# Products of a graph layer from four-pass f32 to three one-pass products, with the order of the engines planned anew

## The chip, the core and the metric

The kernel runs on one core of a Trainium2 chip. The metric is the time in microseconds (us) that the device takes for one execution. A core has five engines with instruction streams of their own: TensorE (PE in the profile; its weight loads are PEld), VectorE (DVE), ScalarE (ACT), GpSimd (POOL) and SyncE (SP, which here only issues transfers). Sixteen DMA engines move data between the device's memory and the core's on-chip memory. Products are summed in the eight banks of PSUM.

## What is computed

One layer of a graph network over 625 nodes with 512 features and 20,625 edges of four relations:

```
h = relu(layernorm(x))                                    # no gain, no bias
msg[e] = (h[src[e]] @ W_rel[type[e]] + b_rel[type[e]]) * w[e]
agg[n] = sum of msg[e] over dst[e] = n, / max(sum of w[e], 1)
x1 = layernorm(h + h @ W_self + b_self + agg) * g1 + b1
y  = x1 + gelu(x1 @ W_ffn1 + b_ffn1) @ W_ffn2 + b_ffn2
out = x + layernorm(y) * g2 + b2
```

All in f32. W_rel is 4 matrices of 512x512, W_self one, W_ffn1 is 512x1024 and W_ffn2 1024x512.

## The kernel before

The nodes stand in 5 blocks of 125 (128 partitions). The work has these stages, each in the profile under the lines given:

- **Splitting the input.** Each block of x is normalized on DVE (L645 to L651), turned by TensorE (L305) and copied to `hT` (L676). The scale of the normalization, `rx`, is left out here and multiplied in when a product is taken from PSUM.
- **Products.** For each relation and each block, `product` (L706) multiplies `hT` by the four 128-row pieces of the relation's matrix `raw[r, k]`, four f32 tiles of 128x128 by 128x512 into one bank; an f32 tile shows as two matmul records. `evict` (L711, ACT) scales the result into the row tile `kept[c]`, and `store_rows` (L337, L338, SP) writes it to `table` in the device's memory. W_self is a fifth relation, `r = R`, with the identity added to it (L698, DVE), and `own_row` (L714, DVE) takes its result, with b_self added, into `z`.
- **Where the edges are.** DVE and indirect transfers find, for each node, the place of its edges in the sorted list (L402 to L539).
- **Blocks 0 to 2** are summed by matrices: `slot_hots` (L578 to L583, DVE) builds bf16 one-hot tiles, `slot_sums` (L594, TensorE) turns them into a weight matrix from the 20 groups of table rows to nodes, `empty_sums` (L600, DVE) takes that from PSUM to `sums_w`, and `chunk_sum` (L937) multiplies it in f32 with the 20 tiles `kept`.
- **Blocks 3 and 4** are summed by gathering: POOL issues 70 gathers of 128 table rows (L818) and 12 more (L872); DVE adds six gathered tiles to a seventh (L842), the sum is cut in a high and a low part (L828 ACT, L832 DVE), and TensorE adds both parts to the nodes by a one-hot matrix in fp32r (L862, L863).
- **Second half.** Statistics of `z` (L968), the power on POOL (L300), `normed` (L974, DVE), turning (L305) and `copy_x1` (L982, ACT, with g1 and b1). The residual is `scaled_z` and `shifted_z` (L985, L988; DVE for blocks 0 to 2, POOL for the others), with b_ffn2 added into the row of b1 (L805). Then, for blocks 0 and 1 together, 2 and 3 together, and 4, the first matrix (L1039), the gelu (L1043, ACT), the second (L1048), the sum and statistics (L1066, L1067), the last scaling and the addition of x and b2, and the store (L1020, L1022).

The order is planned while the program is built. Each piece of work is an `op` with its engine, an assumed duration in us, what it comes after, buffer tokens that it takes and gives, a rank and a lag. `Plan.times` walks through time and gives each engine, whenever it is free, the ready piece of lowest rank; what comes out is each engine's fixed order of instructions. On the chip the engines run these orders in turn, and each waits where its data or buffers are late. Transfers in the plan before have a fixed lag (`lag=2.2` after a load, `LAND = 3.2` after a gather). The gathers come after all stores (`all_stored`), and have `MS = 10` buffers. A rank's first number decides: 0 to 1 for what others wait for, 2 for the products, 3 for the chunk sums, 4 for the last matmuls.

On-chip memory is in 51 row tiles of 128x512 f32 and some larger tiles with tags: `xs` holds the input, then the weight matrix of block 2, then x again for the last addition; `T` and `T1` hold `hT` and later `x1T`; `rows` holds index windows and later the rows of g1, b1, g2 and b2; `w1` and `w2` hold small work tiles and later W_ffn1 and W_ffn2.

Of the kernel before, what the change touches and what calls it, by code (L numbers as in the profile page):

```python
# [68 lines left out]
class Plan:  # L69
# [8 lines left out]
    def op(self, engine, us, fn, after=(), take=(), give=(), lag=0.08, rank=None, order=False, level=None, at=0.0):  # L78
# [3 lines left out]
        if engine == "PE":  # L82
            o.lag = max(lag, self.behind)
        o.after = [(a, a.us if order and a.engine == engine else a.us + (0.0 if a.engine == engine == "PE" else a.lag))
                   for a in after if a is not None]
# [15 lines left out]
    def times(self):  # L101
# [4 lines left out]
        while left:  # L106
# [4 lines left out]
            for o in left:  # L111
                if o.least > t + 1e-6 or free.get(o.engine, 0.0) > t + 1e-6 or any(buffers[k] < o.take.count(k) for k in o.take):
                    continue
                if any(a.at is None or a.at + d > t + 1e-6 for a, d in o.after):
# [13 lines left out]
            if not can:  # L128
                times = [e[0] for e in back] + list(free.values()) + [o.least for o in left]
                times += [max(a.at + d for a, d in o.after) for o in left  # L130
# [6 lines left out]
def gnn_layer(ctx, tc, x, edges, edge_groups, firsts, fourths, windows, w_self, w_rel, w_ffn1, w_ffn2, brel_in, rows_in, cols_in, out, n_edges):  # L137
# [30 lines left out]
    ROWS = 51  # L168

# [30 lines left out]
    brel_4 = const.tile([P, D], F32R, name="brel_4")  # L200
    cols = const.tile([P, KF + 2 * KD], F32, name="cols")
    bf1, g1_T, b1_T = cols[:, :KF], cols[:, KF:KF + KD], cols[:, KF + KD:]
    bself_bc, bf2_bc = row("bself"), row("bf2")
# [10 lines left out]
    raw = {}  # L214
# [52 lines left out]
    def node_constants():  # L267
        place = work.tile([P, 1], F32, tag="place", name="place", bufs=1)
        nc.gpsimd.iota(place, pattern=[[0, 1]], base=0, channel_multiplier=1, allow_small_or_imprecise_dtypes=True)
        nc.gpsimd.memset(node_f, 2.0 * N)  # L270
        nc.gpsimd.memset(xw, -1.0)
# [38 lines left out]
    rx = const.tile([P, NB, 1], F32, name="rx")  # L310
# [166 lines left out]
    def load_brel():  # L477
        for q in range(4):
            nc.sync.dma_start(brel[q * Q:q * Q + R], brel_in[:, :D])
# [6 lines left out]
    def relation_degrees():  # L486
# [7 lines left out]
        nc.vector.tensor_copy(deg_4[:, :, :, :R], deg.unsqueeze(2).to_broadcast([P, INNER, 4, R]))  # L494
# [111 lines left out]
    PARTS = ()  # L606
    ORDER = (0, 1, 2, 3, R)
    MS = 10
    WARM = 10
    GATHER = 1.25  # L610
    LAND = 3.2
    SLACK = 1.2
    LATER = 0.3
    G = 4
    X_AT = [3.55, 5.4, 9.0, 10.7, 10.7]
# [5 lines left out]
    plan = Plan(dict(ps=8, add=3, acc=1, one=2, oh=3, low=2, raw=6, row=ROWS - 7, ms=MS, es=6, ow=4, gT=6), free=dict(SP=9.0), behind=0.6)  # L621
# [6 lines left out]
    op("POOL", 0.7, row_constants, after=[hot_consts], rank=(3, 0), at=9.0)  # L628
# [23 lines left out]

    def x_norm_first(k):
# [5 lines left out]
    def x_root(i):  # L659
        nc.gpsimd.tensor_tensor(rx[:, i, 0:1], mv_x[i][:, 2:3], half, op=ALU.pow)  # L660

    for i in range(NB):
# [4 lines left out]
        else:  # L667
            pieces = [op("DVE", 0.5, lambda i=i: x_norm(i), after=[s], rank=(0, i))]
            z_made[i] = pieces[0]
        root_x[i] = op("POOL", 0.55, lambda i=i: x_root(i), after=[z_made[i]], rank=(0, i))  # L670
# [10 lines left out]
    for n, r in enumerate(ORDER):  # L681
        for k in range(KD):
            if r == 0:
                w_at[r, k] = op("DMA", 0.0, None, at=W_AT[k])
            else:
                w_at[r, k] = op("SP", 0.95, lambda r=r, k=k: load_w(r, k), take=["raw", "row"], lag=2.2, rank=(1, n))
        if n == 1:
            ed_at = op("SP", 1.3, lambda: nc.sync.dma_start(ed, edges), rank=(1, 0.5), lag=2.2)
            brel_at = op("SP", 0.3, load_brel, rank=(1, 2.2), lag=2.2)
            brel_high = op("ACT", 0.65, lambda: nc.scalar.copy(brel_4, brel), after=[brel_at], rank=(2, 0))  # L690
            brel_split = op("DVE", 0.65, low_brel, after=[brel_high], rank=(2, 0))
            op("SP", 0.4, bias_rows, rank=(1, 3.2))
            bself_at = op("SP", 0.9, lambda: load_rows(bself_bc, 5, 6), rank=(1, 3.3), lag=2.2)
            bf2_at = op("SP", 0.9, lambda: load_rows(bf2_bc, 4, 5), rank=(1, 4.4), lag=2.2)
            cols_at = op("SP", 0.1, lambda: nc.sync.dma_start(cols, cols_in), rank=(1, 4.5), lag=2.2)

    def added_ident(k):
        nc.vector.tensor_add(raw[R, k][:, k * P:(k + 1) * P], raw[R, k][:, k * P:(k + 1) * P], ident)  # L698

    ident_w = [op("DVE", 0.2, lambda k=k: added_ident(k), after=[w_at[R, k]], rank=(0.8, k)) for k in range(KD)]  # L700
# [7 lines left out]
    def evict(i, r, box):  # L708
        c = r * NB + i
        new_rows(c)  # L710
        nc.scalar.activation(kept[c][:NG], box["p"][:NG], AF.Copy, scale=rx[:NG, i, 0:1])  # L711

    def own_row(i, box):
        nc.vector.scalar_tensor_tensor(z[:, i, :], box["p"], rx[:, i, 0:1], bself_bc, op0=ALU.mult, op1=ALU.add)  # L714

    own, stored, made_row, used = {}, {}, {}, {}
    for n, r in enumerate(ORDER):
        for i in range(NB):
            box, m = {}, None
            last = i == NB - 1  # L720
            for k0, k1 in ((0, 2), (2, 4)) if (r, i) != (0, 0) else [(k, k + 1) for k in range(KD)]:
                needs = [w_at[r, k] for k in range(k0, k1)] if r != R else [ident_w[k] for k in range(k0, k1)]
                needs += [turned_h[j] for j in turned_h if j[0] == i and (i or j[1] <= k1)]
                m = op("PE", 0.86 * (k1 - k0), lambda i=i, r=r, k0=k0, k1=k1, box=box: product(i, r, k0, k1, box),
                       after=[m, *needs], take=["ps"] if k0 == 0 else [],
# [560 lines left out]
```

## Time and profile before

| | us |
|---|---|
| Median of 3 runs (lowest to highest) | 250.5 (250.49 to 251.59) |
| The profiled execution's own time | 252.5 |
| Its span, from first to last instruction | 250.7 |
| PE busy | 236.6 |
| PEld busy | 131.6 |
| DVE busy | 186.7 |
| ACT busy | 53.7 |
| POOL busy | 130.0 |

Busy time is the union of an engine's instructions. Issuing a transfer from SP isn't counted as busy; an indirect transfer issued by POOL is. The span lies 1.8 us under the execution's own time. The mean granted clock of TensorE over the span is 0.99. A row of the timeline has the start, the length, the engine, the line, the operation, what it writes and reads, how many instructions were merged, and in brackets the idle time before it with what ended it.

### The profile page before, as it was taken

How to read it: one execution, taken by the hardware profiler on the slowest of the kernel's cores; microseconds unless marked ns; L12 is line 12 of the kernel's file. 1: busy time of each engine (PE TensorE's matmuls, PEld its weight loads, DVE VectorE, ACT ScalarE, POOL GpSimd, SP SyncE). 2: the span in 40 equal slices, each digit the busy share in tenths (PEclk: the TensorE clock that was granted, in tenths of full speed). 3: DMA queues.
4: the chain of work that ended last, by engine and by line, in shares of the span. 5: the costliest groups of instructions: out<-in, count | busy, mean ns of one | idle time of the engine just before them, and what ended most of it. 6: DMA issues, size and time to landing. Idle time of an engine off the chain costs nothing. (4 is left out here: it accounts for less than half of the span.)

```text
span 250.7 us, 2873 instructions
## 1 busy us (share of the span) xinstructions
PE 236.6 (94%) x893; PEld 131.6 (52%) x893; DVE 186.7 (74%) x392; ACT 53.7 (21%) x105; POOL 130.0 (52%) x153
## 2 busy tenths in 40 slices
PE   6999989999999999997999999999999999899980
PEld 2554444556555554543444444448954588446850
DVE  7997599999999999958979777887767773222032
ACT  2423242121111111010212201305431331302400
POOL 6487103000000008777778778878777889944400
PEclk9999999999999999999999999999999999999996
DMA  6877931789421214699776766669877650201101
GB/s 219 309 256 189 304 104 46 241 292 343 121 91 41 82 43 117 186 332 394 242 213 199 207 199 176 177 180 324 264 204 214 195 165 0 82 0 41 43 3 45
DMA packets 17991, 43.15 MB, mean 172 GB/s; under 512 B 3002, under 2 KB 3748, under 8 KB 17844
## 3 DMA queue, kind: packets, MB, share of 16 engines
q0 software_dynamic: 7024, 22.27, 29.9%
q1 hardware_dynamic: 10546, 20.32, 24.5%
q10 hardware_dynamic: 402, 0.34, 0.5%
q8 instruction: 8, 0.13, 0.2%
q14 instruction: 11, 0.09, 0.1%
HBM read 36.51 MB, written 6.52 MB: 172 GB/s over the span
## 5 line engine op out<-in xcount | busy, mean ns | idle before, releaser
L818 POOL DMA_INDIRECT ms<-table,row_i x70 | 70.1, 1001 | 73.3 <-DMA table<-m 53.1
L706 PE MATMUL pt<-w,hT 128*128 128x512 f32 x200 | 89.8, 596 | 0.0
L706 PEld LDWEIGHTS pt<-w,hT 128*128 128x128 f32 x200 | 36.6, 191 | 38.9 <-issue 37.5
L937 PE MATMUL acc<-m,sums_w 126*128 126x512 f32 x120 | 53.2, 593 | 0.0
L842 DVE SCALAR_TENSOR_TENSOR ea<-ms,wgt_g,ea 128x512 f32<-128x512 f32 x59 | 43.8, 752 | 12.0 <-DMA ms<-table,row_i 11.3
L937 PEld LDWEIGHTS acc<-m,sums_w 126*128 126x128 f32 x120 | 22.5, 190 | 25.0 <-issue 24.4
L1039 PE MATMUL pu<-x1T,w_sb 128*128 128x250 f32 (+1 forms) x192 | 35.4, 341 | 0.0
L1048 PE MATMUL po<-w_sb,gT 128*125 128x512 f32 (+2 forms) x96 | 35.0, 521 | 0.0
L1039 PEld LDWEIGHTS pu<-x1T,w_sb 128*128 128x128 f32 x192 | 31.5, 191 | 4.4 <-issue 1.9
L600 DVE TENSOR_REDUCE sums_w<-bank 126x160 f32<-126x480 f32 x48 | 28.0, 652 | 0.0
L711 ACT ACTIVATE m<-pt,rx 125x512 f32<-125x512 f32 x20 | 13.8, 688 | 59.8 <-PE pt L706 57.1
L1048 PEld LDWEIGHTS po<-w_sb,gT 128*125 128x125 f32 x96 | 16.8, 188 | 16.3 <-issue 13.8
L1066 DVE TENSOR_TENSOR y<-po,z 125x512 f32<-125x512 f32 (+2 forms) x6 | 3.6, 603 | 23.8 <-PE po L1048 23.8
L594 PEld LDWEIGHTS <-w_first 128*128 128x128 bf16 x192 | 14.0, 147 | 6.4 <-issue 5.6
L583 DVE TENSOR_TENSOR w_first<-eqs,turned 128x640 bf16<-128x640 bf16 x36 | 15.5, 487 | 0.4
L824 ACT ACTIVATE ea<-ms,ed 128x512 f32<-128x512 f32 x10 | 6.9, 694 | 39.4 <-DMA ms<-table,row_i 39.4
L1043 ACT ACTIVATE gT<-pu,cols 128x250 f32<-128x250 f32 (+1 forms) x24 | 10.1, 433 | 21.2 <-PE pu L1039 16.8
L578 DVE TENSOR_TENSOR w_first<-turned,grid 128x2000 bf16<-128x2000 bf16 x12 | 14.3, 1194 | 0.0
L594 PE MATMUL bank<-w_first 128*128 128x120 bf16 x192 | 14.0, 225 | 0.0
L872 POOL DMA_INDIRECT ms_first<-table,x_row x12 | 12.1, 1012 | 3.7 <-issue 3.0
L828 ACT CAST eh<-ea 128x512 fp32r<-128x512 f32 x9 | 5.3, 586 | 34.8 <-DVE ea L842 34.8
L300 POOL TENSOR_TENSOR mv_y<-mv_y,half 125x1 f32<-125x1 f32 x5 | 2.8, 562 | 14.6 <-DVE mv_y L295 14.5
(161 smaller groups left out, 194.7 us busy)
## 6 DMA issues: line engine op xcount, KB each, us to landing
table<-m SPq DMA_DIRECT2D x20, 224.0 KB
w<-in_L_gnn_W_rel_dram SPq DMA_DIRECT2D x16, 256.0 KB
w_sb<-in_L_gnn_W_ffn_dram SPq DMA_DIRECT2D x4, 1024.0 KB
x_late<-in_x_dram SPq DMA_DIRECT2D x1, 1280.0 KB
ms<-table,row_i POOLq DMA_INDIRECT x70, 3.8
w<-in_L_gnn_W_self_dram SPq DMA_DIRECT2D x4, 256.0 KB
late_rows<-in_rows_dram SPq DMA_DIRECT2D x1, 1024.0 KB
out_dram<-y SPq DMA_DIRECT2D x4, 224.0 KB
```

Of the source, the lines that this page charges most:

```text
L578: nc.vector.tensor_tensor(low[:, :, :NG, :], of[:, 0].rearrange("p (a t) -> p a t", t=TB).unsqueeze(2).to_broadcast([P, nb_, NG, TB]), gri ...
L583: nc.vector.tensor_mul(high[:, :, a * HB:(a + 1) * HB, :], eqs, pairs(2 + a))
L594: nc.tensor.matmul(p[:, i * W:(i + 1) * W], low[:, t // TB, :, t % TB], high[:, t // TP, :, t % TP], start=True, stop=True)
L600: nc.vector.tensor_reduce(sums_w[OUTER[d]][:NG + 1, :, n0:n0 + 2 * QT].rearrange("p c (t h) -> p t h c", h=2), p[:NG + 1, :QT * 3 * HB].re ...
L706: nc.tensor.matmul(box["p"], hT[i][:, k, :], raw[r, k], start=(k == 0), stop=(k == KD - 1))
L711: nc.scalar.activation(kept[c][:NG], box["p"][:NG], AF.Copy, scale=rx[:NG, i, 0:1])
L818: nc.gpsimd.indirect_dma_start(out=ms[j], out_offset=None, in_=table[:, :], in_offset=bass.IndirectOffsetOnAxis(ap=row_i[:, j:j + 1], axis=0))
L842: nc.vector.scalar_tensor_tensor(to, ms[j], wgt_g[:, k, q - 1:q], box["sum"], op0=ALU.mult, op1=ALU.add)
L872: nc.gpsimd.indirect_dma_start(out=ms[-b, q], out_offset=None, in_=table[:, :], in_offset=bass.IndirectOffsetOnAxis(ap=x_row[:, b - B0, q: ...
L937: nc.tensor.matmul(acc[b,], sums_w[b][:NG + 1, c, :], kept[c][:NG + 1], start=first, stop=last)
L1039: nc.tensor.matmul(p[:, :self.n], w1_sb[0][:, k, f * P:(f + 1) * P], self.x1T()[:, k, :self.n], start=(k == 0), stop=(k == KD - 1))
L1048: nc.tensor.matmul(p[:at.stop - at.start, :c.stop - c.start], self.gT[f][:, at], w2_sb[0][:, f, c], start=(f == 0), stop=(f == KF - 1))
```

## The change

The products of relations 2, 3 and W_self for all blocks, and of relation 1 for blocks 2 to 4, are formed from three fp32r products each. The high parts hh (h/4095, rounded to fp32r) and wh (about W, rounded) and the low parts hl = h − 4095·hh and wl = W·4096/4095 − wh are made of each tile. Three products are summed in one bank: hh·wh and hl·wl (`product_ends`), and (hh−hl)·(W−wh) (`product_middle`). Their sum is h·W/4095. The factor is taken out at the eviction by a second column of `rx`. The high parts are made on ACT, the low parts on DVE. Each difference is made in two steps: ACT writes the negative of one operand, and a transfer issued by POOL adds the other in memory (`added`, a `dma_start` with `accum_op`). The identity is added to W_self in the same way instead of on DVE. hh lies in the tile `xs`, so the weight matrix of block 2 has to wait for the last product with it (`h_done`); the differences of W of relation 3 lie in the tile `rows`.

The sum of b_ffn2 and b1 enters the last matmuls as one fp32r product (`biases_r` by `brel_4`), which replaces `shifted_z` and the sum of both rows. `normed` moves from DVE to ACT, the residual's scaling and the addition of b2 to x move to DVE for all blocks.

In the plan, each transfer now has a length `dma` on one shared resource, in the order of issue; the lag of its op ends where that resource is through with it, plus 1.3 us. The long loads (W_ffn1, W_ffn2, late rows, x again) are cut in pieces of 256 KB. `MS` is 12, and many ranks and lags are new constants.

```diff
@@ Plan
+        self.moved = 9.0
...
+                if o.dma:
+                    self.moved = max(self.moved, t + o.us + 0.9) + o.dma
+                    o.lag = max(o.lag, self.moved + 1.3 - t - o.us)
@@ loads and constants
+    PARTS = (1, 2, 3, R)
+    LATE_ROWS = 3
+    WHOLE = {1: 2}
+    def in_parts(r, i):
+        return r in PARTS and i >= WHOLE.get(r, 0)
...
-    MS = 10
+    MS = 12
...
+        nc.gpsimd.tensor_tensor(rx[:, i, 1:2], rx[:, i, 0:1], base_of, op=ALU.mult)
...
-        nc.vector.tensor_add(raw[R, k][:, k * P:(k + 1) * P], raw[R, k][:, k * P:(k + 1) * P], ident)
+    def added(to, of):
+        nc.gpsimd.dma_start(to, of, accum_op=ALU.add)
+    ident_w = [op("POOL", 1.05, lambda k=k: added(raw[R, k][:, k * P:(k + 1) * P], ident), after=[w_at[R, k]], rank=(0.8, 0, k), dma=0.6)
+               for k in range(KD)]
@@ splitting
+    def high_h(i):
+        if not h_high:
+            h_all.append(const.tile([P, NB, KD, P], F32R, tag="xs", name="hh"))
+        h_high[i] = h_all[0][:, i]
+        nc.scalar.activation(h_high[i], hT[i], AF.Copy, scale=HIGH)
+    def low_h(i):
+        h_low[i] = row(f"hl_{i}", F32R, (P, KD, P))
+        nc.vector.scalar_tensor_tensor(h_low[i], h_high[i].bitcast(F32), -BASE, hT[i], op0=ALU.mult, op1=ALU.add)
+    def minus_h(i):
...
+            nc.scalar.activation(h_diff[i], h_low[i].bitcast(F32), AF.Copy, scale=-1.0)
+    def diff_h(i):
+        added(h_diff[i].bitcast(F32), h_high[i].bitcast(F32))
+    def high_w(r, k):
+        w_high[r, k] = row(f"wh_{r}_{k}", F32R)
+        nc.scalar.activation(w_high[r, k], raw[r, k], AF.Copy, scale=SHIFT * HIGH)
+    def low_w(r, k):
+        w_low[r, k] = row(f"wl_{r}_{k}", F32R)
+        nc.vector.scalar_tensor_tensor(w_low[r, k], raw[r, k], SHIFT / BASE, w_high[r, k].bitcast(F32), op0=ALU.mult, op1=ALU.subtract)
+    def minus_w(r, k):
...
+            nc.scalar.activation(w_diff[r, k], w_high[r, k].bitcast(F32), AF.Copy, scale=-1.0)
+    def diff_w(r, k):
+        added(w_diff[r, k].bitcast(F32), raw[r, k])
+    def product_ends(i, r, k0, k1, box):
...
+            nc.tensor.matmul(box["p"], h_high[i][:, k, :], w_high[r, k], start=(k == 0), stop=False)
+            nc.tensor.matmul(box["p"], h_low[i][:, k, :], w_low[r, k], start=False, stop=False)
+    def product_middle(i, r, box):
+        for k in range(KD):
+            nc.tensor.matmul(box["p"], h_diff[i][:, k, :], w_diff[r, k], start=False, stop=(k == KD - 1))
@@ order of the hot tiles
-        needs = [z_made[NB - 1]] if d == 2 else []
+        needs = list(h_done.values()) if d == 2 else []
...
-               after=[h, turned_f[d], hot_consts], take=["low"], rank=(3, i), lag=1.0)
+               after=[h, turned_f[d], hot_consts], take=["low"], rank=(SUMS, HOTS * i + HOTS_0), lag=1.0)
...
-                                      give=["ms", "row"], rank=(2, n)))
+                                      give=["ms", "row"], rank=(SUMS, n)))
@@ loads of the second half
+    for k in range(KF):
+        w2_at.append(op("SP", 0.5, lambda k=k: load_w2(k), after=[w2_at[-1]], rank=(2.5, k), lag=SPREAD, dma=LOAD))
...
-    shifted = {b: op("POOL", 1.25, lambda b=b: nc.gpsimd.tensor_add(x_late["x"][:, b, :], x_late["x"][:, b, :], b2_bc()),
+        shifted[b] = op("DVE", 0.67, lambda b=b: nc.vector.tensor_add(x_late["x"][:, b, :], x_late["x"][:, b, :], b2_bc()),
@@ second half
-        nc.vector.tensor_scalar(ow["x1", b], z[:, b, :], t[:, 0:1], t[:, 3:4], op0=ALU.subtract, op1=ALU.mult)
+        nc.scalar.activation(ow["x1", b], z[:, b, :], AF.Identity, bias=t[:, 2:3], scale=t[:, 3:4])
...
-        eng.tensor_add(z[:, b, :], z[:, b, :], b1_bc())
...
+            if not f0:
+                nc.tensor.matmul(p, biases_r[:, :at.stop - at.start], brel_4[:, c], start=True, stop=False)
```

More of the change, by code (lines that the diff above doesn't have):

```diff
@@ L129, in times @@
                 times = [e[0] for e in back] + list(free.values()) + [o.least for o in left]
-                times += [max(a.at + d for a, d in o.after) for o in left
+                times += [max(a.at + a.us + (0.0 if same else a.lag) for a, same in o.after) for o in left
                           if o.after and all(a.at is not None for a, _ in o.after)]
@@ L619, in gnn_layer @@
     together = [[b, b + 1] for b in range(0, NB - 1, 2)] + [[NB - 1]]
-    plan = Plan(dict(ps=8, add=3, acc=1, one=2, oh=3, low=2, raw=6, row=ROWS - 7, ms=MS, es=6, ow=4, gT=6), free=dict(SP=9.0), behind=0.6)
+    plan = Plan(dict(ps=8, add=3, acc=1, one=2, oh=3, low=2, raw=6, row=ROWS - 6, ms=MS, es=6, ow=4, gT=6), free=dict(SP=9.0), behind=0.6)
     op = plan.op
@@ L627, in gnn_layer @@
     hot_consts = op("POOL", 2.9, hot_constants, rank=(0.5, 0))
[L628 removed]
+    row_consts = op("POOL", 0.7, row_constants, after=[hot_consts], rank=(3, 0), at=9.0)
     def warm():
@@ L708, in evict @@
     def evict(i, r, box):
-        c = r * NB + i
+        c, q = r * NB + i, int(in_parts(r, i))
         new_rows(c)
-        nc.scalar.activation(kept[c][:NG], box["p"][:NG], AF.Copy, scale=rx[:NG, i, 0:1])
+        nc.scalar.activation(kept[c][:NG], box["p"][:NG], AF.Copy, scale=rx[:NG, i, q:q + 1])
     def own_row(i, box):
[L714 to L725, printed above, removed]
-                       give=["raw", "row"] * (k1 - k0) if last else [], rank=(2 if r != R else 2.5, n, i, k0), lag=0.3)
-            used[r, i] = m
-            if r < R:
-                e = made_row[r, i] = op("ACT", 0.69, lambda i=i, r=r, box=box: evict(i, r, box), after=[m, root_x[i]], take=["row"], give=["ps"],
-                                        rank=(1, n, i))
-                stored[r, i] = op("SP", 0.95, lambda c=r * NB + i: store_rows(c), after=[e], rank=(0.8, n, i), lag=2.5)
-            else:
-                own[i] = op("DVE", 0.68, lambda i=i, box=box: own_row(i, box), after=[m, bself_at, root_x[i]],
-                            give=["ps"] + (["row"] if last else []), rank=(0.6, n, i))
```

273 lines of the change are left out of this document (195 added, 78 removed).

## The prediction

> **What bounds the kernel now.** I read first the stretches between the points where TensorE changes its kind of work, all engines side by side (columns: length, then busy time and instructions of PE, weight loads, DVE, ACT, POOL; then granted clock, DMA share, GB/s).
>
> ```profile
> 0.00:7.00 7.00, 4.94 (x14) 2.23 (x14) 5.20 (x22) 1.72 (x4) 4.05 (x16) 1.00 0.68 226
> 7.00:33.00 26.00, 25.97 (x74) 12.14 (x73) 20.72 (x69) 7.52 (x15) 14.03 (x22) 1.00 0.82 262
> 33.00:94.00 61.00, 59.72 (x289) 32.17 (x288) 59.81 (x135) 12.41 (x21) 1.96 (x2) 1.00 0.43 138
> 94.00:110.00 16.00, 16.00 (x66) 8.16 (x65) 15.93 (x28) 1.38 (x2) 12.62 (x12) 1.00 0.63 188
> 110.00:169.00 59.00, 56.95 (x149) 26.36 (x148) 46.89 (x76) 9.18 (x18) 45.82 (x47) 1.00 0.74 227
> 169.00:204.00 35.00, 34.41 (x132) 23.71 (x131) 25.67 (x43) 12.35 (x26) 27.46 (x32) 1.00 0.76 236
> 204.00:244.00 40.00, 38.60 (x179) 26.82 (x177) 10.39 (x20) 9.15 (x21) 23.50 (x24) 1.00 0.12 36
> ```
>
> From 7 to 244 us PE is busy 231.7 of 237 us (25.97+59.72+16.00+56.95+34.41+38.60), at full granted clock. It sets the end. DVE is nearly as full from 33 to 110 (75.7 of 77) and has room after (73 of 94, then 10 of 40). So PE time is worth its full length, unless DVE or the transfers step into its place. The chain view is no help: it holds only the last 1.3 us. What PE does comes from the groups of instructions (busy time, mean ns):
>
> ```profile
> L706 PE MATMUL pt<-w,hT 128*128 128x512 f32 x200 | 89.8, 596 | 0.0
> L937 PE MATMUL acc<-m,sums_w 126*128 126x512 f32 x120 | 53.2, 593 | 0.0
> L818 POOL DMA_INDIRECT ms<-table,row_i x70 | 70.1, 1001 | 73.3 <-DMA table<-m 53.1 <-issue 12.4 <-DMA ms<-table,row_i 3.7
> L842 DVE SCALAR_TENSOR_TENSOR ea<-ms,wgt_g,ea 128x512 f32<-128x512 f32 x59 | 43.8, 752 | 12.0 <-DMA ms<-table,row_i 11.3
> ```
>
> Each of the 100 f32 tiles of the products at L706 shows as two records. The mean of 596 ns holds latency that overlaps; the price is the step from start to start, in TensorE's timeline:
>
> ```profile
> 16.05 17.33 PE L706 MATMUL pt<-w,hT 128*128 128x512 f32 x40
> 33.22 1.00 PE L561 MATMUL tf<-ident_b,fields 128*128 128x128 bf16 x15
> ...
> 200.71 0.58 PE L862 MATMUL acc<-eh,oh 128*128 128x512 f32 x1
> 201.13 0.40 PE L863 MATMUL acc<-el,oh 128*128 128x512 f32 x1
> 201.36 1.85 PE L1039 MATMUL pu<-x1T,w_sb 128*128 128x250 f32 x8
> ```
>
> Forty records in 33.22−16.05 = 17.17 us: 0.429 each, 0.858 us for one f32 tile. The edge sums (L862, L863) already use fp32r, the kind to which the change goes: from L863 to the next start is 0.23 us, from L862 to L863 0.42.
>
> **The change, part by part.**
>
> *Products.* Relations 2, 3 and W_self (5 blocks each) and 3 blocks of relation 1 are 18 blocks of 4 tiles: 72 of the 100 tiles go from one f32 product to three fp32r ones. An fp32r pass costs at least half an f32 record, 0.2145, as such a record covers two passes if one f32 tile is four of 512 columns; at most 0.42, where L862 still waits for its forerunner's streaming. I take 0.22, beside the 0.23 that follows L863, as that step has nothing in front of it. Per tile 0.858 − 3×0.22 = 0.198; times 72 = 14.3 us off PE. At 0.23 it is 12.1, at 0.2145 15.5; at 0.286 nothing is left. (The Trainium skill, "TensorE: Matmul & The Clock Gate", section "Wait — 56ns, not 53.3ns?", gives one warm pass of 512 columns as 215.7 ns from start to start; by it, an estimate, the gain would be 72×(0.858−0.647) = 15.2 us. The 0.23 of the trace is a little above.)
>
> *Biases by TensorE.* The last matmuls get one fp32r product of 512 columns for each of 5 blocks (block 4 in two cuts of 384 and 128): 5×0.22 = 1.1 us more on PE, in its packed last stage. The DVE and POOL additions that this replaces were hidden.
>
> *Splitting h and W.* The durations, here and in the next part:
>
> ```profile
> L711 ACT ACTIVATE m<-pt,rx 125x512 f32<-125x512 f32 x20 | 13.8, 688 | 59.8 <-PE pt L706 57.1 <-POOL node_row L288 2.7
> L974 DVE TENSOR_SCALAR x<-z,mv_z 128x512 f32<-128x512 f32 x5 | 4.0, 803 | 4.3 <-POOL mv_z L300 4.2
> L985 DVE TENSOR_TENSOR z<-x,late_rows 128x512 f32<-128x512 f32 x3 | 2.1, 707 | 0.0
> L745 DVE CAST ident_b<-ident 128x128 bf16<-128x128 f32 x1 | 1.9, 1865 | 0.0
> L698 DVE TENSOR_TENSOR w<-w,ident 128x128 f32<-128x128 f32 x4 | 1.0, 285 | 0.0
> ```
>
> ACT: 5+5 passes over h, 16+16 over W, at the 0.69 of the evictions = 29 us between 12 and about 75. Evictions and copies hold 20 of its 87 us from 7 to 94, so it fits. DVE: 5+16 subtractions of 128x512 at 0.75 (the L842 row) = 15.8 us.
>
> *Moved between engines.* DVE gains 5 additions to x_late and 2 scalings (7×0.7 = 4.9). It loses 5 normalizations, now ACT (4.0), 3 shifts and one bias addition (4×0.7 = 2.8), 4 ident additions (1.0) and the ident copy (1.9). With the splits DVE is up by about 11 us, 186.7 to 198. POOL loses some 11 us of elementwise work late and gains 25 accumulating DMAs early, at the 1.0 of a gather's issue = 25 us, where it is busy 1.96 of 61 us.
>
> *Accumulating DMAs.* No row of before shows one. Bounds: a plain 256 KB transfer, and twice that, since it reads two operands:
>
> ```profile
> q0 software_dynamic: 7024, 22.27, 29.9%
> q1 hardware_dynamic: 10546, 20.32, 24.5%
> DMA to landing us min/median/max: 3.4/3.8/8.4
> ```
>
> Queue 0 moves 22.27 MB in 0.299×250.7 = 75 us: 0.88 us for 256 KB, so 0.88 to 1.76 each. The tight place is 7 to 33 us, with 0.82×26 = 21.3 us of transfers already: seven accumulates (4 for W of relation 1, 3 for h) want 6.2 to 12.3 us of the 4.7 left, so 1.5 to 7.6 us late. PE has whole tiles until about 33 and then the first two passes of three blocks (3×8×0.22 = 5.3), so some 2.6 us of the longer delay are covered behind the 3.8 of a landing. Stall of PE: 0 to 5 us; below nothing only if PE's present gaps close. I take 1.5, near the lower end, as the queue's price for the nearest kind of transfer is the lower one. The other 14 accumulates come at 4 or 5 per relation (11.3 us of PE for 5 blocks, 20×0.66, less hot sums between), over a DMA share of 0.43, from which the 3 MB of late rows and W_ffn1 can move later.
>
> *Order: gathers.* They are the second chain. POOL issues them back to back from the last stored row to the end:
>
> ```profile
> 91.30 0.39 SPq L338 DMA_DIRECT2D table<-m  x1
> ...
> 94.02 0.94 POOL L818 DMA_INDIRECT ms<-table,row_i  x1 [53.11 <-DMA table<-m]
> 95.27 1.95 POOL L818 DMA_INDIRECT ms<-table,row_i  x1 [0.30 <-issue]
> ...
> 202.53 0.95 POOL L818 DMA_INDIRECT ms<-table,row_i  x1 [0.30 <-issue]
> ...
> 210.90 0.15 DVE L295 TENSOR_SCALAR mv_z<-mv_z 128x1 f32<-128x1 f32 x1
> ...
> 215.75 1.50 ACT L982 ACTIVATE x1T<-tp_x,cols 128x125 f32<-128x125 f32 x4 [0.19 <-PE tp_x L305]
> ...
> 229.28 7.30 PE L1039 MATMUL pu<-x1T,w_sb 128*128 128x125 f32 x64
> ```
>
> The chain of block 4 is done at 217.3, and PE wants it at 229.3: 12 us of slack. PE gains 13.2 us net, so the gathers must start 1.2 us earlier to stay hidden. The 13 converted blocks of relations 1 to 3 give 13×4×0.198 = 10.3 us before the last stored row; 4 W_self loads with their accumulates (rank 0.8) may be queued before the first gather on POOL, 8×1.0 = 8 us at worst. Slack left 9 us, or 1. Cost: nothing; if the cover is gone, each us late is a us of the end. The loads that the change cuts into 256 KB pieces add some 17 issues on SP at 0.35 to 0.45 (7 us of a queue that mostly waits for ACT's evictions).
>
> *What of DVE.* Busy by 204 is 174.2, with the 4 or so to the last statistics 178, and some 9 to 11 of the new work comes earlier: 188. It must be over by 210.9+12−13.2 = 209.7. Less 0.8 at the start and 5 us of early waits for x and the windows, that leaves 16 us in which it may idle. Before it idled 12.1 from 110 to 169, 9.3 from 169 to 204. Taken as covered, with little to spare.
>
> **Sum.** −14.3 + 1.1 + 1.5 = −11.7 us. The profiled execution (span 250.7, 252.5 with what lies around it) would become 240.8; it stands 2.0 above the median of the runs, 250.5, so I forecast 238.8.
>
> **The rivals.**
>
> *Transfers set the first stage* (0.20). Accumulates at 1.76 us and stores, loads and windows in the same stretch: PE stalls the 5 us bounded above, and as much again (2 to 3 us) for a second relation whose W comes late: −13.2 + 5 to 8 = 242.3 to 245.3. For it: share 0.82 from 7 to 33 at 262 GB/s. Against: 0.43 after. The 1.95 of the gather at 95.27, beside 0.94 a step before, is a POOL issue held up while DVE built one-hot tiles; 25 new issues stand in that stage. (The Trainium skill, "SBUF — State Buffer", section "Who interferes with whom", lets DVE and GpSimd block each other fully on a shared port pair, for DVE operations with two SBUF inputs against GpSimd reads; the 1.95 agrees. By the row each accumulate would land 1 us later, which speaks for this rival.)
>
> *DVE becomes the bound: the side of no gain* (0.10). Row sums, one-hot tiles and splits stand in one fixed queue; a row sum placed ahead of its gather's landing holds up the one-hot sums of block 2, and with them the chunk sums on PE. Those of block 2 moreover must now wait for the last W_self product, since they take the same memory as the split h. Each us of idling over 16 is a us of the end: it cancels the 11.7 from 28 us on, and with 30 to 32 the time is 238.8+14 to 16 = 252.8 to 254.8. Against: before, those waits were 21 us. It decides only if they grow by a third.
>
> *The passes are not at streaming rate* (0.05). Weight loads of 190 ns stand before every pass, against 0.22:
>
> ```profile
> L863 PEld LDWEIGHTS acc<-el,oh x9: 186/191/193, 120.1 to 200.9; 128*128 128x128 f32 x9
> ```
>
> If they don't overlap fully and a pass takes 0.286, the 72 tiles gain nothing, and 250.5+1.1 = 251.6, or about 250 if half a us of gaps closes. Against: the f32 records of 250 columns at L1039 keep 32 to 6.75 us (0.211) with the same loads:
>
> ```profile
> 201.36 6.91 PE L1039 MATMUL pu<-x1T,w_sb 128*128 128x250 f32 x32
> 208.11 1.02 PE L865 MATMUL acc<-es,oh 128*128 128x512 f32 x2
> ```
>
> *More than forecast* (0.10): pass at 0.2145, no stall, and the gaps of PE in the middle (237−231.7 = 5.3) partly closed: 250.5 − 15.5 + 1.1 − 2 = 234.1.
>
> **How the numbers follow.** The forecast has 0.55 (235.5 to 241.5), the rivals 0.20, 0.10, 0.05 and 0.10. The likeliest gives 238.8. The range 234 to 246 leaves out the DVE rival, most of the 0.05 and a bit of the first and last: under 0.2. A change of under 0.5% (1.25 us) can't be told from none by these runs (250.49 to 251.59). Faster: 0.55+0.20+0.10, and 0.01 of the DVE rival = 0.86; within 0.5%: 0.05; slower 0.09.
>
> **What would show it.** Right: fp32r products at L706's place with 0.215 to 0.23 from start to start; PE busy down to about 223; the first gather from POOL at about 77 to 85; W_self products over by 97; no wait of PE over 1 us for a DMA between 33 and 60; block 4's x1T ready before PE asks. Wrong: PE idle "<-DMA" for the differences of W or h; DVE idle over 16 us before the last statistics with PE waiting at the chunk sums; weight loads that PE waits for; gathers starting after 92.

## The result, and the profile after

The changed kernel is slower: 259.2 us (median of 4 runs, 257.7 to 259.5) against 250.5 us before, a ratio of 1.033 [1.028, 1.038]. Forecast were 238.8 us and a range of 234 to 246. The profiled execution of after has a span of 257.7 us and takes 259.5 by itself.

The stretches of after beside those shown of before (length; then busy time and instructions of PE, weight loads, DVE, ACT, POOL; granted clock, DMA share, GB/s):

```profile
7.00:33.00 26.00, 26.00 (x74) 12.33 (x74) 22.84 (x66) 10.13 (x22) 14.13 (x25) 1.00 0.68 211
33.00:94.00 61.00, 50.89 (x260) 39.34 (x259) 44.46 (x106) 30.81 (x57) 27.06 (x28) 0.89 0.96 199
94.00:110.00 16.00, 14.85 (x87) 11.88 (x86) 13.79 (x25) 0.69 (x1) 8.95 (x9) 1.00 0.89 288
110.00:169.00 59.00, 58.25 (x212) 29.54 (x212) 57.83 (x101) 10.81 (x20) 39.28 (x41) 0.97 0.64 190
169.00:204.00 35.00, 35.00 (x127) 23.10 (x126) 28.09 (x46) 10.95 (x23) 27.39 (x31) 1.00 0.73 229
```

The damage lies between 33 and 94 us. PE has 50.89 of 61 us there (before 59.72), at a granted clock of 0.89 (before 1.00). DVE too has only 44.46 (before 59.81), so DVE isn't the engine that is full there. The DMA share went from 0.43 to 0.96. What PE waited for (total, times, longest):

```profile
PE pt L820 <- DMA wd<-w: 4.1, 4, 1.8
PE tf L584 <- ACT m L756: 3.2, 1, 3.2
...
PE pt L815 <- ACT turned L589: 1.9, 1, 1.9
PE acc L1019 <- DVE es L996: 1.7, 1, 1.7
```

In PE's timeline the passes and the gaps stand side by side. L815 and L816 are the passes `hh` by `wh` and `hl` by `wl`, L820 is `hd` by `wd`:

```profile
37.19 1.26 PE L584 MATMUL tf<-ident_b,fields 128*128 128x128 bf16 x10 [3.19 <-ACT m L756]
...
43.81 0.63 PE L815 MATMUL pt<-wh,hh 128*128 128x512 f32 x1
44.23 0.63 PE L816 MATMUL pt<-wl,hl 128*128 128x512 f32 x1
...
49.09 2.37 PE L820 MATMUL pt<-wd,hd 128*128 128x512 f32 x9 [0.71 <-DMA wd<-w]
...
53.37 0.40 PE L815 MATMUL pt<-wh,hh 128*128 128x512 f32 x1
...
56.84 0.39 PE L816 MATMUL pt<-wl,hl 128*128 128x512 f32 x1
...
59.61 0.50 PE L820 MATMUL pt<-wd,hd 128*128 128x512 f32 x1 [1.22 <-DMA wd<-w]
61.87 4.21 PE L820 MATMUL pt<-wd,hd 128*128 128x512 f32 x9 [1.76 <-DMA wd<-w]
```

Fifteen steps from 53.37 to 56.84 are 0.231 us each: that is the price of a pass at full clock. At 43.81 it is 0.42, and nine passes at 61.87 take 4.21 us: after each group of gaps the granted clock drops (it is 0.50 from 38 to 40, from 44 to 46 and from 62 to 66 us), and some two dozen passes cost 0.2 us more each, about 5 us. (The Trainium skill, "TensorE: Matmul & The Clock Gate", section "Part 1: The HAM clock gate", describes this: an idle TensorE is gated to half its clock until it has been busy for a few us again. The half rate agrees, 0.42 against 0.231; the idle window of about 3.4 us that the section gives is longer than any single gap here.) So one us of waiting costs more than a us: beside the 10.1 us in which PE is idle (61 − 50.89) stand these 5.

The twelve `hd` by `wd` passes of relation 1 are over by 51.5 us, and waited 0.71 us for a transfer. The longer waits for `wd`, 1.22 and 1.76, are at the next group of them, those of relation 2.

Behind the 3.2 us wait for an eviction (`m`) stands a row of ACT's timeline:

```profile
32.81 1.15 ACT L783 ACTIVATE hd<-hl 128x512 fp32r<-128x512 f32 x2 [11.15 <-PE pt L751]
```

ACT stood still for 11.15 us at the rounding of a negative of h, until the whole products (L751) were over. The cause is a buffer. `turned_tile` gives the tiles of two blocks one memory under the tag `T`, and a new tile under that tag takes the memory of the oldest. The differences `hd` are wanted first for blocks 2 and 3, but get the memory of `hT` of blocks 0 and 1, which the whole products of relation 1 still read. The plan makes `minus_h` wait for the pair of the same number (`used[last_whole[j], j] for j in pair`), not for the one whose memory it gets. Behind ACT's wait are queued the evictions, and the high and negative parts of W. POOL's queue stands still with it, as the transfer that adds to `hd` comes ahead of the rest of its work:

```profile
33.74 2.62 POOL L742 DMA_DIRECT2D hd<-hh  x2 [8.94 <-ACT hd L783]
```

The search of the edges of blocks 3 and 4 (L428, L407 before) goes on behind that at 36.67, in place of 24.22 before.

The accumulates, first in the groups by duration (POOL's issue: busy time, mean ns), then in the page's queues and issues (median us to landing):

```profile
L742 POOL DMA_DIRECT2D wd<-w x12 | 16.2, 2231 | 0.0
```

```profile
q0 software_dynamic: 12160, 28.04, 44.4%
...
wd<-w POOLq DMA_DIRECT2D x12, 256.0 KB, 9.1
```

An issue takes 2.2 us of POOL (forecast 1.0), a landing 9.1 us. Last, the gathers:

```profile
98.61 1.07 POOL L972 DMA_INDIRECT ms<-table,row_i  x1 [18.51 <-DMA w_sb<-in_L_gnn_W_ffn_dram]
...
220.81 0.95 POOL L972 DMA_INDIRECT ms<-table,row_i  x1 [0.30 <-issue]
```

They start at 98.61 in place of 94.02. From the first gather to the end of the span it is 159.1 us (before 156.7): of the 7.0 us by which the span grew, 4.6 came before that point and 2.4 after it.

### The profile page after: what moved, and what is told of

Same layout as the page of the kernel before. It is cut to its first block, busy times and chain, and to the rows that moved or that the text cites. A ratio compares the mean times of both kernels' runs of the same rounds, so it can differ in the third digit from the quotient of the medians.

```text
span 257.7 us, 3225 instructions
## 1 busy us (share of the span) xinstructions
PE 234.2 (91%) x971; PEld 149.6 (58%) x971; DVE 194.9 (76%) x406; ACT 78.5 (30%) x154; POOL 149.3 (58%) x183
## 3 DMA queue, kind: packets, MB, share of 16 engines
q0 software_dynamic: 12160, 28.04, 44.4%
## 4 chain that ended last, share of the span: by engine, by line
PE 73%; DMA 12%; POOL 4%; DVE 4%; issue 3%; ACT 2%; SPq 0%; POOLq 0%; DVEq 0%; ACTq 0%
PE acc L1092 21%; PE pu L1195 13%; PE po L1207 11%; PE pt L751 9%; DMA wd<-w 7%; PE pt L820 4%; DMA ms<-table,row_i 4%; PE bank L617 3%; PE pt L815 3%; PE pt L816 2%; PE warm L666 2%; DMA table<-m 2%; POOL ms L972 1%; POOL wd L742 1%; POOL hd L742 1%
## 5 line engine op out<-in xcount | busy, mean ns | idle before, releaser
L972 POOL DMA_INDIRECT ms<-table,row_i x70 | 72.4, 1035 | 39.5 <-DMA w_sb<-in_L_gnn_W_ffn_dram 18.5
L815 PE MATMUL pt<-wh,hh 128*128 128x512 f32 x72 | 31.3, 435 | 1.9 <-ACT turned L589 1.9
L816 PE MATMUL pt<-wl,hl 128*128 128x512 f32 x72 | 30.0, 417 | 0.0
L1207 PEld LDWEIGHTS po<-w_sb,gT 128*125 128x125 f32 x96 | 16.7, 188 | 15.2 <-issue 12.8
L751 PE MATMUL pt<-w,hT 128*128 128x512 f32 x56 | 25.0, 594 | 0.0
L820 PE MATMUL pt<-wd,hd 128*128 128x512 f32 x52 | 16.5, 445 | 4.1 <-DMA wd<-w 4.1
L815 PEld LDWEIGHTS pt<-wh,hh 128*128 128x128 f32 x72 | 14.7, 204 | 5.9 <-ACT turned L589 2.6
L617 PE MATMUL bank<-w_first 128*128 128x120 bf16 x192 | 15.2, 228 | 2.8 <-DVE w_first L606 1.5
L751 PEld LDWEIGHTS pt<-w,hT 128*128 128x128 f32 x56 | 10.2, 190 | 11.3 <-issue 10.3
L794 DVE SCALAR_TENSOR_TENSOR wl<-w,wh 128x512 fp32r<-128x512 f32 x16 | 10.6, 690 | 8.1 <-DMA wd<-w 7.0
L816 PEld LDWEIGHTS pt<-wl,hl 128*128 128x128 f32 x72 | 14.7, 204 | 3.4 <-issue 0.2
L742 POOL DMA_DIRECT2D wd<-w x12 | 16.2, 2231 | 0.0
```

The costliest lines, as they stand in the source:

```text
L617: nc.tensor.matmul(p[:, i * W:(i + 1) * W], low[:, t // TB, :, t % TB], high[:, t // TP, :, t % TP], start=True, stop=True)
L742: nc.gpsimd.dma_start(to, of, accum_op=ALU.add)
L751: nc.tensor.matmul(box["p"], hT[i][:, k, :], raw[r, k], start=(k == 0), stop=(k == KD - 1))
L815: nc.tensor.matmul(box["p"], h_high[i][:, k, :], w_high[r, k], start=(k == 0), stop=False)
L816: nc.tensor.matmul(box["p"], h_low[i][:, k, :], w_low[r, k], start=False, stop=False)
L820: nc.tensor.matmul(box["p"], h_diff[i][:, k, :], w_diff[r, k], start=False, stop=(k == KD - 1))
```

## The experiments

Two suspects stood after that: the hidden wait for a buffer, and the accumulates. The first four kernels ran on one chip with the kernel before at 250.52 us.

**A memory of its own for each pair of blocks.**

```diff
-            return const.tile([P, KD, 2 * P], dtype, tag="T", name=f"{name}_{b}", bufs=NB // 2)
+            return const.tile([P, KD, 2 * P], dtype, tag=f"T{b // 2}", name=f"{name}_{b}")
```

> The changed kernel with a tag of its own for each pair of blocks, so that the difference of h of blocks 2 and 3 lies where their own turned h lay, and not where that of blocks 0 and 1 lies. Order and plan unchanged. Theory T (transfers: an accumulating transfer costs 1.8 us per 256 KB, the stage from 40 to 62 us is saturated, TensorE waits and its clock falls): only ScalarE's wait of 11.2 us goes, TensorE still waits for differences; 255 to 259 us. Theory S (slot: ScalarE, held 11 us behind a tile that the plan believed free, sends the work behind it in one burst): TensorE's waits between 33 and 70 us and the clock's fall go, 243 to 249 us.

Measured (e1): 250.57 us, 0.9985 [0.9948, 1.0022], so 8.6 below the change, and between the two ranges that were expected: neither suspect is the only one. ACT's long wait is gone. The stretch, and the largest of PE's waits that is left:

```profile
33.00:94.00 61.00, 56.02 (x308) 44.27 (x307) 54.70 (x126) 23.50 (x43) 22.94 (x24) 0.94 0.97 220
```

```profile
PE pt L820 <- DMA wd<-w: 3.7, 2, 1.9
```

PE has 56.0 of 61 us, and the only transfers that it waits for are those of `wd`.

**Plain copies in place of the accumulates.** The additions are left out.

```diff
-        nc.gpsimd.dma_start(to, of, accum_op=ALU.add)
+        nc.gpsimd.dma_start(to, of)
```

> The changed kernel with the 25 accumulating transfers as plain copies of the same sizes from the same queue; the additions are left out. T: the share of the transfers on their queue falls by about 20 us of 16 engines, landings from a median of 7.8 us to 4 or 5, TensorE's waits for them go: 246 to 251 us. S: the burst behind ScalarE's wait stays, 254 to 258 us.

Measured (e2): 250.59 us, 0.999 [0.9948, 1.0032], 8.6 below the change as well, and with the other wait still there. ACT's waits, POOL's groups and the page of this kernel:

```profile
ACT hd L783 <- PE pt L751: 11.4, 1, 11.4
```

```profile
L742 POOL DMA_DIRECT2D wd<-w x12 | 6.8, 574 | 2.2 <-ACT wd L806 1.8 <-issue 0.4
```

```profile
q0 software_dynamic: 8832, 28.04, 36.7%
...
wd<-w POOLq DMA_DIRECT2D x12, 256.0 KB, 5.8
```

The same bytes now land in 5.8 us, POOL issues one in 0.57 us, and PE waits for no `wd`. The time is in the range that was expected if the transfers were the loss, but it is no more than half of the loss.

**The differences formed by POOL**, with no accumulates, and the identity added by DVE as before.

```diff
-            nc.scalar.activation(h_diff[i], h_low[i].bitcast(F32), AF.Copy, scale=-1.0)
+        nc.gpsimd.tensor_sub(h_diff[i], h_high[i].bitcast(F32), h_low[i].bitcast(F32))
...
-            nc.scalar.activation(w_diff[r, k], w_high[r, k].bitcast(F32), AF.Copy, scale=-1.0)
+        nc.gpsimd.tensor_sub(w_diff[r, k], raw[r, k], w_high[r, k].bitcast(F32))
```

> The changed kernel with each difference as one subtraction by GpSimd (1.27 us for 128x512 in the kernel before) in place of ScalarE's negative and the accumulating transfer; the identity by VectorE again. The order is planned with these. T: no accumulating transfers at all, 245 to 250 us. S: the wait for the tile moves from ScalarE to GpSimd, where it holds the other differences but no evictions: 248 to 254 us.

Measured (e3): 259.47 us, 1.0329 [1.0264, 1.0394], above both ranges. The transfers are relieved (share 0.27 from 33 to 94 us), but another loss took their place:

```profile
L802 POOL TENSOR_TENSOR wd<-w,wh 128x512 fp32r<-128x512 f32 x12 | 17.7, 1497 | 1.5 <-PE pt L812 1.5
...
L793 DVE SCALAR_TENSOR_TENSOR wl<-w,wh 128x512 fp32r<-128x512 f32 x16 | 19.2, 1247 | 0.0
```

DVE's subtraction for `wl` takes 1247 ns in place of 690 in after. (The Trainium skill, "SBUF — State Buffer", section "Who interferes with whom", has a DVE operation with two inputs in SBUF contend with a GpSimd one that reads SBUF; the rows agree.) As the order was planned anew for it, this run does not price the accumulates.

**All else of the change, with no product to base 4095.**

```diff
-    PARTS = (1, 2, 3, R)
+    PARTS = ()
```

> The changed kernel with no product in parts: 100 f32 tiles, no splitting and no accumulating transfers for it, all else (order, transfers as a shared resource, biases by TensorE, moves between engines) as in the change. T and S alike: near the kernel before, 249 to 253 us. If the new order or the moves themselves cost (theory O): 255 us or more.

Measured (e4): 252.28 us, 1.0057 [1.0018, 1.0096]. New order, biases and moves together cost 1.8 us by the medians (0.5 to 2.4 by the interval). This kernel also gives the accumulates their price:

```profile
q0 software_dynamic: 7600, 22.53, 30.4%
```

Over its span of 249.0 us queue 0 takes 75.7 us; with 21 plain copies of 256 KB 36.7% of 247.8 = 90.9; with 21 accumulates 44.4% of 257.7 = 114.4. So, as an estimate, a copy costs 15.2/21 = 0.72 us of the 16 engines, an accumulate 38.7/21 = 1.84. (This kernel still accumulates the identity, four times 64 KB, where the kernel with plain copies copies it; counted in proportion, that makes the copy 0.78.)

**Both suspects away, and three other ways out.** A first set of these kernels, and later a first set of the three that follow, ran where the kernel before itself took 276.6 and 276.9 us; their profiles have stretches of up to 18 us in which no transfer moved. Their times (274.8, 284.5, 267.0, 267.4; then 272.2, 267.1, 273.7 us) aren't used. What was expected of them:

> Both edits together: a tag of its own for each pair of blocks, and the accumulating transfers as plain copies (the additions are left out). If the wait for the tile and the price of the transfers are two losses that add up (each edit alone gained 8.6 us): 242 us or less. If they are one loss, work bunched behind a wait that meets transfers too slow to catch up, so that either cure does: 247 to 250 us, and what is left is elsewhere (VectorE and the gathers).

> The tags, and in the plan the measured length of an accumulating transfer, 1.85 us, in place of 1.0; all the work is the same, its order is planned with it. If TensorE's waits come from an order built on a wrong price: 243 to 247 us. If from the transfers' load itself, which no order takes away: 249 to 252 us.

> As the run before (tags, price 1.85), with relation 1 whole: 60 tiles in parts in place of 72, and 17 accumulating transfers of 256 KB in place of 21. TensorE has 12 x (0.858 - 3 x 0.231) = 2.0 us more work, the transfers 7.4 us less, ScalarE 5.5 and VectorE 2.8 less. If the load of the transfers binds the first stage: 241 to 246 us. If TensorE's work binds: 2 us above the run before.

> As the run before, with the five differences of h by one VectorE subtraction each: 9 us less of transfers early, 3.5 us more of VectorE. If transfers still bind: 1 to 3 us below the run before. If VectorE binds by now: 1 to 4 us above it.

The same four kernels, beside the kernel before at 250.31 us:

> Edit: e1_slots with plain copies in place of the accumulates (the additions left out), so both suspects gone. If the hidden wait for the pairs' memory and the accumulates' price are two separate losses, it falls by both, 8.6 us each: 259.2 - 17.2 = 242 us, near the 238.8 us forecast and the 11.9 us that the passes save. If they are one loss (either alone frees the same idle of TensorE, and the end is then set by VectorE and the gathers), it stays at 249 to 251 us.

Measured (e12): 242.15 us, 0.9632 [0.9579, 0.9686]. Against the change it is 17.0 less, so the two losses add up: 8.6 for the buffer, 8.4 for the accumulates (250.57 − 242.15). The stretch, and POOL's first gather:

```profile
33.00:94.00 61.00, 59.98 (x350) 48.27 (x349) 59.35 (x134) 24.20 (x44) 21.73 (x28) 1.00 0.77 248
```

```profile
81.45 1.00 POOL L972 DMA_INDIRECT ms<-table,row_i  x1 [18.61 <-DMA w_sb<-in_L_gnn_W_ffn_dram]
```

PE is full at full clock, although relation 1 is in parts, and the gathers start 17 us earlier than in after.

Pairs' own memory, and the accumulate's price in the plan:

```diff
-    ADD, LOAD, STORE, FETCH = 1.0, 0.75, 0.7, 0.85
+    ADD, LOAD, STORE, FETCH = 1.85, 0.75, 0.7, 0.85
```

> Edit: e1_slots with the accumulate's measured price in the plan, all products to base 4095 kept. Theory A (the plan under-priced the accumulates, and so packed them where the transfers could not follow): below e1_slots's 250.57 by most of its 5 us of idle TensorE between 33 and 70 us: 244 to 248 us. Theory B (21 accumulates of 1.84 us are too much for the first stage in any order): within 1.5 us of e1_slots.

Measured (e11): 251.89 us, 1.0059 [1.0015, 1.0103]: a planner that knows the price finds no better order for all 72 tiles.

The same, and relation 1 whole again:

```diff
-    PARTS = (1, 2, 3, R)
+    PARTS = (2, 3, R)
...
-    WHOLE = {1: 2}
+    WHOLE = {}
```

> Edit: the pairs' own memory (as in e1_slots), an accumulate priced by the plan as measured (1.85 us of the 16 engines for 256 KB in place of 1.0), and relation 1 whole again: 60 steps' worth of products to base 4095 in place of 72, with 16 accumulates in place of 21 in the first stage. Theory A (what is left of the loss in e1_slots is the accumulates: late `wd` and a full queue between 33 and 70 us, 32.0 of 37 us of TensorE busy there): with a quarter fewer of them and an order that knows their price, TensorE has at least 36 of 37 us there, and the time falls below e1_slots's 250.57 us although 12 tiles x 0.165 us = 2.0 us of TensorE work come back: 243 to 247 us. Theory B (the end is set by the gathers and VectorE after 94 us whatever the first stage does): 250 to 252.5 us.

Measured (e9): 241.33 us, 0.9596 [0.9529, 0.9663], below the 243 to 247 that were expected. (Accumulates of 256 KB are 17 in place of 21 over the whole kernel; the count in the expectation was wrong.)

That, and the fine part of h by DVE (`H_ON_DVE = True`):

> Edit: e9_two_less, and the fine part of h formed by one VectorE subtraction (0.69 us by the rows of wl) in place of ScalarE's negative and an accumulate: no accumulate of h is left (8 of w remain). Theory A: the transfers are relieved again (5 accumulates x 1.1 us above a plain copy = 5.6 us of the 16 engines), VectorE gets some 3.5 us more in a stage where it has 0.5 to 6 us idle; 240 to 246 us, at or below e9_two_less, no TensorE wait above 1 us for a transfer of w or h between 33 and 94 us. Theory B (VectorE is the bound): 1 to 3.5 us above e9_two_less.

Measured (e10): 241.62 us, 0.9627 [0.9568, 0.9686]: the same as e9. With relation 1 whole, five accumulates fewer make no difference.

**Which of the edits does it.** First the expectations of the set that isn't used, then those of the same kernels beside the kernel before at 251.33 us.

> Edit: the change as it is, with relation 1 whole again and nothing else: the pairs still share one rotating memory, the plan still prices an accumulate at 1.0. Theory A (two losses that add up, each of some 8.5 us: the wait for the pairs' memory, and the accumulates of relation 1): only the second goes, 248 to 252 us, and ScalarE still waits some 10 us for a whole product before it can write a rounded h. Theory B (fewer accumulates are enough, the wait for the memory does no harm where the transfers have room): 241 to 244 us, as e9_two_less.

> Edit: e9_two_less with the plan's old price of an accumulate (1.0 in place of 1.85), so the pairs' own memory and relation 1 whole. Theory A (the number of accumulates in the first stage decides, 13 in place of 17, and their price in the plan does not, as e11_price against e1_slots says): 240 to 244 us. Theory B (the right price is needed for the fewer accumulates to help): 246 to 251 us, with waits of TensorE for `wd` above 2 us.

> Edit: e11_price (all 72 tiles to base 4095, the pairs' own memory, price 1.85) with the fine part of h formed by VectorE, so 12 accumulates in the first stage in place of 17 and 12 tiles more in passes than e10_two_less_h. Theory A (the accumulates were the loss, not the products of relation 1): the 2.0 us that the 12 tiles save in passes come in full, 238.5 to 243 us, no TensorE wait above 1 us for a transfer between 33 and 70 us. Theory B (relation 1 is the first to be multiplied, and its parts come too late whatever forms them, or VectorE with 5 subtractions more is the bound): 246 to 252 us.

> The change with relation 1 whole again and nothing else (pairs' memory shared, old price). The first run of this kernel was disturbed by stretches of 5 to 10 us in the gathers in which no transfer moved (the kernel before took 276.85 us there), but its first stage had TensorE busy for 36.6 of the 37 us between 33 and 70 us. Theory A (the accumulates and the products of relation 1's parts are what the first stage could not bear; the shared memory then does no harm): 241 to 244 us. Theory B (the shared memory still costs its 8.5 us): 248 to 252 us.

Measured (e16): 242.04 us, 0.963 [0.9573, 0.9687]. Relation 1 whole is enough by itself, with the shared memory and the old price. Its stretch, and PE's timeline (L751 are whole products):

```profile
33.00:94.00 61.00, 59.74 (x337) 44.36 (x336) 59.27 (x131) 24.20 (x44) 26.89 (x28) 1.00 0.97 227
```

```profile
15.92 19.05 PE L751 MATMUL pt<-w,hT 128*128 128x512 f32 x44
...
36.04 7.08 PE L751 MATMUL pt<-w,hT 128*128 128x512 f32 x16
...
43.18 1.88 PE L751 MATMUL pt<-w,hT 128*128 128x512 f32 x4
46.76 1.10 PE L820 MATMUL pt<-wd,hd 128*128 128x512 f32 x4
...
65.61 1.09 PE L820 MATMUL pt<-wd_late,hd 128*128 128x512 f32 x4
```

The reader should set this beside after, where the whole products end and the first difference is used here:

```profile
15.44 17.33 PE L751 MATMUL pt<-w,hT 128*128 128x512 f32 x40
...
47.51 0.86 PE L820 MATMUL pt<-wd,hd 128*128 128x512 f32 x3
```

The transfers are as full as in after (0.97 against 0.96), and the first difference is used at 46.76 against 47.51, hardly sooner. But PE has whole tiles until 45.06 in place of 32.77. The 12 tiles of relation 1, 12×0.858 = 10.3 us whole, are work under which parts can be made. The change turned just these into something that needs parts itself. That this cover, and not the four accumulates that are spared, is what helps is argued here, not shown. It isn't the only way out either: in e12 PE is as full with relation 1 in parts. ACT's wait of 11 us goes too: `hd` is asked for at 33.90, when the products that read its memory are done. By the code, relation 2 begins with blocks 0 and 1, so the first `hd` gets the memory of the very pair for which the plan makes it wait, and the shared tag does no harm in this order.

> e9_two_less with the plan's old price of an accumulate. Theory A (the price in the plan does not matter): 240 to 244 us. Theory B (it does): 246 to 251 us.

Measured (e17): 242.19 us, 0.9648 [0.9591, 0.9706], as e9: the price in the plan doesn't matter here.

> All 72 tiles to base 4095, the pairs' own memory, the fine part of h on VectorE: 12 accumulates in the first stage. Theory A (the number of accumulates was the loss): 238.5 to 243 us. Theory B (relation 1's parts come too late whatever forms them, or VectorE is the bound): 246 to 252 us. In the disturbed run TensorE was busy for 36.0 of 37 us between 33 and 70 us and 22.9 of 24 to 94 us, which leaves 2 us of loss in the first stage and speaks for A with 242 to 244 us.

Measured (e18): 248.39 us, 0.9899 [0.9838, 0.9959]. It has one accumulate fewer than e16 (16 of 256 KB) and the pairs' own memory, but all 72 tiles, and it misses the 238.5 to 243. Few gaps of PE are left before 94 us (58.94 of 61), yet the gathers start only at 89.93:

```profile
34.06 0.17 DVE L447 CAST at_i<-at_f 128x2 int32<-128x2 f32 x1
34.50 1.28 POOL L428 DMA_INDIRECT rows_first<-in_windows_dram,at_i  x1 [9.29 <-DMA w<-in_L_gnn_W_rel_dram]
...
80.40 4.74 PE L820 MATMUL pt<-wd_late,hd 128*128 128x512 f32 x20
...
81.52 0.69 ACT L756 ACTIVATE m<-pt,rx 125x512 f32<-125x512 f32 x1 [16.27 <-PE pt L820]
```

PE worked, but at the wrong things: the last passes of relation 3, which the last stored rows need, come for all five blocks at once at 80.40. In e16 they begin at 65.61. The differences of W of relation 3 lie in the tile of the index windows, and so come after the search of the edges, which stood on POOL for 9.29 us here. The profile puts that down to a load of W, but L428 reads `at_i`, which DVE had ready only at 34.23. The differences of relation 3 are issued from 64.41 on (e16: 57.30). That this order is the reason for the 6 us above e16 is read from the trace; no run took it alone. With relation 1 in parts and five accumulates fewer than in after, PE waits for no difference here, so the lack of whole products isn't what makes this kernel slow. The runs don't part cleanly what relation 1 left whole gives as cover from what it spares in parts.

## Why the prediction was wrong

*The pass* was sized at 0.22 us, beside a row of 0.23, and is 0.231. Per tile 0.858 − 0.693 = 0.165, times 72 = 11.9 us in place of 14.3: 2.4 us too much hoped for. "At 0.23 it is 12.1" was the term. It is right as a mechanism: with 60 tiles 9.9 us, less the 1.8 that the rest of the change costs, make 8.1, and the four kernels with relation 1 whole measured 8.7 to 9.3 under the kernel before.

*Order, biases and moves*: 1.1 forecast for the biases and nothing for the order, 1.8 measured for all of it (e4). Nearly right.

*The accumulates' price* was bounded by 0.88 and 1.76, with a plain transfer's end taken "as the queue's price for the nearest kind of transfer". It is 1.84, above both ends, about 2.5 times the same copy's 0.72, and 2.2 us of POOL in place of 1.0. The end that counts two operands was the nearer one, and the other was taken.

*The stall of PE*, "0 to 5 us", of which it took 1.5: this is the step that failed. Measured are 17.0 us (259.2 − 242.15), half of it the buffer and half the accumulates. Two things were not in it. The first is the wait for `hT`'s memory. The bound counted what the transfers need and took ACT as free ("it fits", by the sum of its busy time). It named no wait that the change adds on ACT and nothing that queues behind it, although the pair of tiles and its tag stand in the code; no row of before could show the wait. The second is the landing. "PE has whole tiles until about 33" was read rightly from the trace, and set against a landing of 3.8 us (the 2.6 us of cover beside it stand without their working; 5.3 less 3.8 is 1.5). Landings took 9.1 us, and after 33 us nearly all that PE had to do needed parts. The long waits came at relation 2, whose accumulates the prediction let pass free over a share of 0.43; from 33 to 94 us the share was 0.96. With the same transfers as plain copies and no wait for the buffer (e12) PE had 59.98 of 61 us.

*The sum.* 250.5 − 11.9 + 1.8 = 240.4 would be the change without its two losses. Measured without them were 242.15: 1.8 us remain, whose cause isn't shown. That kernel takes 2.6 us longer from the first gather to the end than before (240.7 − 81.45 = 159.3 against 156.7).

*Gathers*: their start, at 77 to 85 if the forecast was right and after 92 if it was wrong, was the right sign to watch. From the first gather to the end of the span it takes 156.7 us before, 159.1 after, 156.9 in e1, 156.6 in e18, 159.3 in e12 and 155.3 in e16. These differ by 4.0 us, while the starts lie 17.2 us apart (81.45 to 98.61). So the start of the gathers, hence the end of the first stage, makes most of the difference in time; not all, as e12 and e16 start 4.1 us apart and take the same.

*The rivals.* "Transfers set the first stage" named half of the cause at 5 to 8 us, and rightly "a second relation whose W comes late". What it lacked was the drop of the clock behind gaps and a second cause beside it. "DVE becomes the bound" was not what happened: DVE idled 16.5 of 61 us between 33 and 94. It was full from 110 to 169 (57.83 of 59), but PE was idle for only 0.75 us there. "The passes are not at streaming rate" asked for 0.286; they ran at 0.231.

*A faster version.* The one with relation 1 whole and nothing else (e16) is 17 us below the change and 9 below the kernel before. Of the versions run, 241.33 (e9) is the lowest; 241.33 to 242.19 can't be told apart.

The signs: PE busy was forecast at 223 and is 234.2; without the two losses (e12) it is 227.6. The two waits over 1 us for `wd` before 62 us are the first sign named as wrong. W_self's products were to be over by 97 and run to about 109.

## What to carry to other kernels

Before a product is made cheaper by splitting its operands, look at what PE does while the parts are made, and price how long a part takes to land. Where it lands late, leave the first products whole: here that gave back 17 us for 2 us of passes, though the runs don't show by which of its effects. Where a tile gets its memory from a rotating tag, find whose memory it gets, and put that reader into the list of what it comes after; the sum of an engine's busy time doesn't show a wait that stands at the head of its queue. And bound a stall by what stands behind it on each engine, with the slow passes that follow a gap, not by the transfer alone.

## What was not expected of the hardware

By the shares of queue 0, an accumulating transfer within on-chip memory took 1.84 us of the 16 engines for 256 KB, a copy of the same bytes 0.72. Those into `wd` landed in 9.1 us at the median, as copies in 5.8. A gap of 3.2 us and groups of gaps of 0.4 to 1.9 us were enough for passes of 0.42 us in place of 0.23. A full share of the transfers by itself cost nothing: from 33 to 70 us in e9 it was 1.08, and PE was busy throughout.

```profile
33.00:70.00 37.00, 37.00 (x197) 26.17 (x196) 35.70 (x89) 20.42 (x39) 21.39 (x21) 1.00 1.08 217
```
